# Moving a small expert product to the last group of heads, and its rows to the last three blocks

## The chip, the core and the metric

The kernel runs on one NeuronCore of a Trainium2 chip. Its engines work side by side, each through its own instructions in order: TensorE (PE in the profile; its weight loads are PEld), VectorE (DVE), ScalarE (ACT), GpSimd (POOL) and SyncE (SP, which only issues DMAs here). The metric is the device time of one execution in microseconds: 4233.94 us as the median of three runs, 4232.88 to 4234.31.

## The reference

The input x has 4 batches of 2048 tokens of 512 numbers. Its layer norm `xn` goes into two parts, and both are added to x:

```python
x = x + attention(xn) + experts(xn)

# attention: 16 heads of 32; q and k pass a filter over frequencies
scores = einsum('bhqd,bhkd->bhqk', q, k) / sqrt(32)
out = softmax(scores) @ v
attention = out @ w_out + b_out

# experts: each token goes to its best of 8, the first 100 tokens of each are kept
dispatched = einsum('tec,th->ech', dispatch, hs).reshape(800, 512)
expert_out = dispatched @ w_expert + b_expert     # one matrix for all experts
combined = combine.reshape(-1, 800) @ expert_out  # each row times its gate, back to its token
```

So the experts are 800 rows, 7 tiles of 128, through one 512 by 512 matrix. All else is attention in float32.

## The kernel before, in words

Heads are taken in groups of four; with four batches that makes 16 groups, k = 0 to 15 (group 12 is the first of the last batch). A group has four **blocks** of 512 queries, and a block has 16 **halves**, one for each tile of 128 keys. So there are 1024 halves, and `start = k * GH` with GH = 64 is the first half of group k. Two halves make a **window**.

In each half PE computes the scores of four heads (`scores`), ACT their exponentials into a tile `even` or `odd`, and PE the product of the half before with the values (`products`), which DVE adds to `num`. The row maxima must be known ahead: PE also computes the scores of a later block (`max_matmuls`), DVE reduces them (`max_reduce`, to `part`). These run 20 halves ahead, so that the last 20 halves have none. When the maxima of a block are complete, `max_negate` (DVE), `max_close` (PE and ACT) and `max_split` (POOL, tiles `rest` and `row`, then three DMAs on SP to `negm`) make a row of shifts from them, and `shift` puts it into the score banks at half 0 of the block, with PE products of `negm`. In a window the order is: `max_split` if due, then `heads` (the `divide` of a block: POOL computes `ot` from `num` and `factor`), then `pair` (a DMA on POOL's queue that adds the tile `odd` to `even`, 1 MB), then `add_to` (the sums of an older window, two additions on POOL, or on DVE when no maxima are left), then the two halves.

Everything else is laid into an **agenda** of halves: `at(half, step, cost=...)`. The cost counts PE work in units of one **piece**, a projection of 128 tokens (`query_key` or `value`): 32 instructions of 128*32 with 128 columns, in four column tiles, evicted by ACT. Each group makes the projections of the next one, 48 pieces, and `spread` places them in order, each as early as it may, while the sum of costs stays under a level times the number of halves; it takes the lowest level that fits. Pieces of keys (`kinds == 1`) may not stand before half 32 of a group. `projections(k)` sets their order; for k in CROWDED, which is (1, 14), two blocks of values and one of queries come first, 12 pieces, and then the keys. After each block `close_steps` puts a `fold` in half 5 of the next block, eight reciprocals (`invert`, DVE) in halves 6 to 13, the divide at half 14, four `result` products in halves 1 to 4 of the block after, and in half 5 the DMA that adds `y`, 1 MB, to `out`. For the last block but one they are placed earlier: fold in half 7, the divide and the results from half 12. The last block loads its rows of `out` into `y` (SP) and stores their sums at the end (`close_last`).

The experts (`expert_steps`, from `place_experts`) begin in half 36 of group 12: the matrix `w_exp`, the bias `b_exp` and the tables of chosen tokens are loaded, each row tile is fetched by an indirect DMA on POOL's queue, measured (DVE) and scaled. From half 62 of group 12 on, every second half holds an `expert(i)`: PE multiplies a turned tile by the matrix (four products of 128 by 128, 512 columns), DVE adds the bias, PE turns the next tile, ACT copies, weighs and normalizes. Their costs, 35 in all, mostly stand in group 13. From half 26 of group 13 on there is one row tile a block: `gather_row` reads its rows of `out` (an indirect DMA), `add_row` adds the expert's rows to them on POOL, and `scatter_row` writes them back, two halves apart. All POOL work, DMA issues too, is in program order (`InOrder`), and semaphores order reads and writes of `out`: a gather waits for the landing of the `y` added before it.

Of the kernel before, what the change touches and what calls it, by code (L numbers as in the profile page):

```python
# [21 lines left out]
B, S, DM = 4, 2048, 512  # L22
# [81 lines left out]
def attention_and_top1_experts(ctx: ExitStack, tc: tile.TileContext, a: dict, out: bass.AP):  # L104
# [7 lines left out]
    out_rows = out.rearrange("b s d -> (b s) d")  # L112
# [6 lines left out]
    def bank():  # L119

        return array[:, next(turns), :]
# [20 lines left out]
    ident, upto, same_head = (square[:, j, :] for j in range(3))  # L142
# [47 lines left out]
    on = SimpleNamespace(sync=nc.sync)  # L190
# [227 lines left out]
    def columns(out, lhsT, rhs, **flags):  # L418

        for h in range(HG):  # L420
            at = slice(DH * h, DH * (h + 1))
            on.tensor.matmul(out[at], lhsT=lhsT[:, at], rhs=rhs, **flags)
# [127 lines left out]

    taken = {}

    def expert_steps():


        def begin():
            w_exp = chunk("w_exp")
            on.sync.dma_start(out=w_exp, in_=a["L0_ffn_w_expert"].rearrange("(r p) n -> p r n", p=P))
            b_exp = work.tile([P, DM], F32, tag="b_exp", name="b_exp", bufs=1)
            on.sync.dma_start(out=b_exp, in_=a["L0_ffn_b_expert"].partition_broadcast(P))  # L560
            entries = small.tile([P, NTAB, ST, 2], F32, name="entries")
# [12 lines left out]
            mv = small.tile([P, ST, 2], F32, name="mv1")  # L574
            index = [bass.IndirectOffsetOnAxis(ap=who[:, i : i + 1], axis=0) for i in range(ST)]
            bound = {"bounds_check": B * S - 1, "oob_is_err": False}
            taken.update(mv=mv, w_exp=w_exp, b_exp=b_exp, entry=entry, index=index, bound=bound, xg=xg)

        def row(i):
            return taken["xg"][i // TQ][:, i % TQ, :]  # L580

        def fetch(i):
            on.gpsimd.indirect_dma_start(row(i), None, rows, taken["index"][i], **taken["bound"])

        def measure(i):
            stats = small.tile([P, 6], F32, name="stats1")
            on.vector.bn_stats(stats, row(i))
            on.vector.bn_aggr(taken["mv"][:, i, :], stats)

        def scale():  # L590
            rstd = small.tile([P, ST], F32, name="rstd1")
            on.gpsimd.tensor_scalar(rstd, taken["mv"][:, :, 1], EPS, None, ALU.add)
            on.gpsimd.tensor_tensor(rstd, rstd, power[:, 0:ST], ALU.pow)
            shift = small.tile([P, ST], F32, name="shift1")
            on.gpsimd.tensor_tensor(shift, taken["mv"][:, :, 0], rstd, ALU.mult)
            on.gpsimd.tensor_scalar(shift, shift, -1.0, None, ALU.mult)
            taken.update(rstd=rstd, shift=shift)

        def expert(i):

            if i >= 2:
                at = slice(i - 2, i - 1)
                pe = bank()
                for r in range(NR):
                    on.tensor.matmul(
                        pe,
                        lhsT=taken["xt"][:, r * P : (r + 1) * P],
                        rhs=taken["w_exp"][:, r, :],
                        start=(r == 0),
                        stop=(r == NR - 1),  # L610
                    )
                on.vector.tensor_tensor(row(i - 2), pe, taken["b_exp"], ALU.add)
            if 1 <= i <= ST:
                px = bank()
                for r in range(NR):
                    on.tensor.transpose(px[:, r * P : (r + 1) * P], row(i - 1)[:, r * P : (r + 1) * P], ident)
                taken["xt"] = work.tile([P, QB], F32, tag="byx", name="xt", bufs=1)
                on.scalar.copy(taken["xt"], px)
            if i >= 2:
                on.scalar.activation(row(i - 2), row(i - 2), AF.Copy, scale=taken["entry"][:, at, 1])  # L620
            if i < ST:
                at = slice(i, i + 1)
                on.scalar.activation(
                    row(i), row(i), AF.Identity, bias=taken["shift"][:, at], scale=taken["rstd"][:, at]
                )

        return begin, fetch, measure, scale, expert

    def gather_row(i):
        taken["sum"] = work.tile([P, DM], F32, tag="byx", name="yg", bufs=1)  # L630
        on.gpsimd.indirect_dma_start(taken["sum"], None, out_rows, taken["index"][i], **taken["bound"])

    def add_row(i):
        row = taken["xg"][i // TQ][:, i % TQ, :]
        on.gpsimd.tensor_tensor(row, row, taken["sum"], ALU.add)

    def scatter_row(i):
        row = taken["xg"][i // TQ][:, i % TQ, :]
# [105 lines left out]
    load, measure, scale, normalize, turn, first_route, first_sums, _ = token_stage(0)  # L744
# [8 lines left out]
    for c in range(1, NG):  # L753
        cols = slice(2 * DM + c * P, 2 * DM + (c + 1) * P)
# [63 lines left out]
    for i, item in enumerate(stream[:MAX_AHEAD]):  # L818
# [4 lines left out]
        half = next(turns), next(turns)  # L823
# [16 lines left out]
    HB = NT  # L840
    GH = NQ * HB
# [49 lines left out]
    def place_experts(start):  # L891


        begin, fetch, measure, scale, expert = expert_steps()
        first = start + 36
        at(first, begin)
        for i in range(ST):
            at(first + 2 + 2 * i, fetch, i)
            at(first + 6 + 2 * i, measure, i)
        at(first + 22, scale)  # L900
        for i in range(ST + 2):
            at(first + 26 + 2 * i, expert, i, cost=(NR if i >= 2 else 0) + (1 if 1 <= i <= ST else 0))
        for i in range(ST):
            free = start + GH + i * HB + 26
            for step in (gather_row, add_row, scatter_row):
                at(free, step, i)
                free += 2

    def plan(k):

# [86 lines left out]
    for block in range(1, B * NG * NQ):  # L997

        costs[block * HB - 4] += 0.25
    place_experts((B - 1) * NG * GH)  # L1000
    for k in range(B * NG):
        plan(k)

# [104 lines left out]
```

## Time and profile before

| | us |
|---|---|
| median of three runs | 4233.94 |
| profiled execution, its own time | 4234.09 |
| span of that execution in the trace | 4232.3 |
| PE busy | 4175.4 |
| DVE busy | 3453.9 |
| POOL busy | 2958.5 |
| ACT busy | 2489.9 |

Busy times are shares of the span in which an engine executed something; matmuls are pipelined, so a busy PE is not PE at its peak. The chain of waits follows the work that ended last, back from the last instruction, to what released it each time. A group of instructions has one line, with engine, operation, output and inputs, shapes, count, and mean duration. Nearly all instructions carry one line number, that of a helper, so that they are told apart by their tiles. A stage is a window of time from the span's start, and the windows below are cut at halves: a half begins where ACT starts the first of its two exponentials.

### The profile page before, as it was taken

To read this page: it belongs to the slowest core of one execution; us is meant where nothing else is said; L and a number is where in the kernel's file an instruction comes from. 1 tells how busy PE (TensorE), PEld (TensorE's weight loads), DVE (VectorE), ACT (ScalarE), POOL (GpSimd) and SP (SyncE) were. 2 spreads that over 40 slices of the span, in tenths; PEclk is the share of its full clock that TensorE was granted. 3 is DMA by queue.
4 is the path that set the end of the run, shared out by engine and by line. 5 is a ranking of instruction groups with operands and counts; after the bars stand their busy time and mean duration, and the time that the engine had idled before them with its cause. 6 is when DMAs were issued, how large, how long until landed. Compare 5 with 4: busy or idle time off the path is not lost.

```text
span 4232.3 us, 120483 instructions
## 1 busy us (share of the span) xinstructions
PE 4175.4 (99%) x52270; PEld 1866.6 (44%) x52270; DVE 3453.9 (82%) x5199; ACT 2489.9 (59%) x3411; POOL 2958.5 (70%) x2046
## 2 busy tenths in 40 slices
PE   8999999999999999999999999999999999999998
PEld 4444444444444444444444444444444443444432
DVE  6778888977788888897788888888778888788896
ACT  2555556666565556657565556566656555556665
POOL 1567776776876767776687767767678776677873
PEclk9999999999999999999999999999999999999999
DMA  4767788987787778898677787798777976778788
GB/s 120 154 128 150 157 159 170 209 195 149 142 163 153 156 156 166 181 203 185 134 158 156 157 160 152 159 204 195 166 149 147 182 159 132 152 162 163 157 170 170
DMA packets 183419, 685.95 MB, mean 162 GB/s; under 512 B 26902, under 2 KB 56760, under 8 KB 117608
## 3 DMA queue, kind: packets, MB, share of 16 engines
q0 software_dynamic: 110432, 605.83, 73.0%
q1 hardware_dynamic: 71280, 71.90, 5.5%
q8 instruction: 409, 6.70, 0.6%
q14 instruction: 122, 1.00, 0.1%
q10 hardware_dynamic: 1176, 0.52, 0.0%
HBM read 71.85 MB, written 88.96 MB: 38 GB/s over the span
## 4 chain that ended last, share of the span: by engine, by line
PE 88%; DMA 5%; POOL 3%; DVE 2%; issue 1%; ACT 0%; POOLq 0%; ACTq 0%; DVEq 0%
PE array L84 88%; DMA even<-odd 4%; POOL even L84 2%; DVE part L84 1%; POOL rstd L84 0%; DVE stats L84 0%; DVE num L84 0%; POOL ot L84 0%; DMA odd<-in_L_attn_w_qkv_dram 0%; DVE factor L84 0%; POOL steps_of_keys L84 0%; DMA negm<-row 0%; POOL rest L84 0%; POOL row L84 0%; ACT odd L84 0%
## 5 line engine op out<-in xcount | busy, mean ns | idle before, releaser
L84 DVE TENSOR_REDUCE part<-array 128x1 f32<-128x512 f32 (+1 forms) x3369 | 2496.5, 799 | 675.7 <-PE array L84 671.1
L84 POOL TENSOR_TENSOR even<-even 128x1024 f32<-128x1024 f32 x876 | 2111.2, 2500 | 458.4 <-DMA even<-odd 456.3
L84 PE MATMUL array<-keys,q 32*128 32x512 f32 x8192 | 2085.4, 616 | 8.5 <-DVE part L84 4.9
L84 PE MATMUL array<-q,steps_of_keys 32*128 32x512 f32 x8192 | 2038.9, 618 | 3.6 <-issue 2.1
L84 ACT ACTIVATE odd<-array 128x1024 f32<-128x1024 f32 x1024 | 996.2, 1021 | 489.0 <-PE array L84 366.0
L84 ACT ACTIVATE even<-array 128x1024 f32<-128x1024 f32 x1024 | 995.3, 1022 | 487.3 <-PE array L84 447.5
L84 PEld LDWEIGHTS array<-keys,q 32*128 32x128 f32 x8192 | 787.3, 185 | 583.2 <-DVE part L84 352.5
L84 PEld LDWEIGHTS array<-q,steps_of_keys 32*128 32x128 f32 x8192 | 704.8, 184 | 255.3 <-issue 225.1
L84 POOL DMA_DIRECT2D even<-odd x510 | 456.1, 894 | 436.3 <-ACT odd L84 369.0
L84 DVE TENSOR_TENSOR num<-num,array 128x512 f32<-128x512 f32 x960 | 650.3, 677 | 21.9 <-PE array L84 15.8
L84 PEld LDWEIGHTS array<-xnT,w 128*32 128x32 f32 x15808 | 444.6, 110 | 259.5 <-DVE part L84 165.0
L84 PE MATMUL array<-even,v 128*32 128x512 f32 x4096 | 547.0, 606 | 1.2 <-DVE part L84 1.2
L84 PE MATMUL array<-odd,v 128*32 128x512 f32 x4096 | 547.7, 607 | 0.3 <-DVE part L84 0.3
L84 PE MATMUL array<-xnT,w 128*32 128x128 f32 (+1 forms) x15808 | 522.2, 277 | 0.9 <-ACT xnT L84 0.7
L84 PEld LDWEIGHTS array<-w,xnT 128*32 128x32 f32 x8192 | 230.7, 110 | 146.4 <-DVE part L84 103.5
L84 DVE RECIPROCAL factor<-den 128x64 f32<-128x64 f32 x504 | 274.3, 545 | 0.0
L84 PE MATMUL array<-wo,ot 128*32 128x512 f32 x2048 | 267.1, 594 | 5.0 <-POOL ot L84 5.0
L84 PE MATMUL array<-w,xnT 128*32 128x128 f32 x8192 | 269.3, 273 | 1.3 <-DVE num L84 1.2
L84 PEld LDWEIGHTS array<-odd,v 128*32 128x32 f32 x4096 | 81.0, 108 | 391.2 <-DVE part L84 382.2
L84 PEld LDWEIGHTS array<-even,v 128*32 128x32 f32 x4096 | 80.7, 108 | 391.2 <-DVE part L84 381.4
L84 POOL DMA_DIRECT2D out_dram<-y x63 | 85.3, 1354 | 198.2 <-ACT y L84 126.7
L84 ACT COPY y<-array 128x512 f32<-128x512 f32 x188 | 110.0, 585 | 104.2 <-PE array L84 104.1
(129 smaller groups left out, 1437.5 us busy)
## 6 DMA issues: line engine op xcount, KB each, us to landing
even<-odd POOLq DMA_DIRECT2D x510, 1024.0 KB, 8.1
out_dram<-y POOLq DMA_DIRECT2D x63, 1024.0 KB, 9.8
xs<-in_L_attn_x_dram SPq DMA_DIRECT2D x96, 256.0 KB
out_dram<-in_L_attn_x_dram SPq DMA_DIRECT2D x16, 1024.0 KB
w<-wd SPq DMA_DIRECT2D x45, 256.0 KB
wo<-in_L_attn_w_out_dram SPq DMA_DIRECT2D x16, 256.0 KB
negm<-row SPq DMA_DIRECT2D x192, 4.0 KB
xs<-in_L_attn_x_dram SPq DMA_DIRECT2D x2, 1024.0 KB
```

The source lines that it names most:

```text
L84: done = act(*args, **kwargs)
```

## The change

The experts' product moves from groups 12 and 13 to group 15, the last. It begins in half 34 of group 14. The product of a tile is cut into four quarters of 128 columns, each done as `columns`, four column tiles, in a half of its own; the turn of a tile has its own half too. The halves used are those of group 15 without other products: not halves 1 to 5 of a block. Seven tiles of five halves each take 35 of them: halves 0 and 6 to 15 of blocks 0, 1 and 2, and halves 0 and 6 of block 3. The turned tile lies in buffers of projection weights that group 15 no longer needs. Rows are gathered, added and scattered in halves 8, 10 and 12 of blocks 1 (two tiles), 2 (two tiles) and 3 (three tiles), with a buffer for each gathered tile of a block.

```diff
+    def spent_weights(s):
+        return weights.tile([P, NR, P], F32, name=f"w{s}", bufs=1).rearrange("p r n -> p (r n)")
+
+    def spare_row():
+        return work.tile([P, DM], F32, tag="byx", name="yg", bufs=1)
...
-        def expert(i):
-
-            if i >= 2:
-                at = slice(i - 2, i - 1)
-                pe = bank()
-                for r in range(NR):
-                    on.tensor.matmul(
-                        pe,
-                        lhsT=taken["xt"][:, r * P : (r + 1) * P],
-                        rhs=taken["w_exp"][:, r, :],
-                        start=(r == 0),
-                        stop=(r == NR - 1),
-                    )
-                on.vector.tensor_tensor(row(i - 2), pe, taken["b_exp"], ALU.add)
...
+        def normal(i):
+            at = slice(i, i + 1)
+            on.scalar.activation(
+                row(i), row(i), AF.Identity, bias=taken["shift"][:, at], scale=taken["rstd"][:, at]
+            )
+
+        def turn(i):
+            px = bank()
+            for r in range(NR):
+                on.tensor.transpose(px[:, r * P : (r + 1) * P], row(i)[:, r * P : (r + 1) * P], ident)
+            taken["xt"] = spent_weights(i % 2)
+            on.scalar.copy(taken["xt"], px)
+
+        def multiply(i, quarter):
+            cols = slice(quarter * P, (quarter + 1) * P)
+            pe = bank()[:, cols]
+            for r in range(NR):
+                columns(
+                    pe,
+                    taken["xt"][:, r * P : (r + 1) * P],
+                    taken["w_exp"][:, r, cols],
+                    start=(r == 0),
+                    stop=(r == NR - 1),
                 )
+            on.vector.tensor_tensor(row(i)[:, cols], pe, taken["b_exp"][:, cols], ALU.add)
+
+        def weigh(i):
+            on.scalar.activation(row(i), row(i), AF.Copy, scale=taken["entry"][:, i : i + 1, 1])
...
     def gather_row(i):
-        taken["sum"] = work.tile([P, DM], F32, tag="byx", name="yg", bufs=1)
-        on.gpsimd.indirect_dma_start(taken["sum"], None, out_rows, taken["index"][i], **taken["bound"])
+        taken["sum", i] = spare_row() if i % 2 else spent_weights(2 if i < ST - 1 else 1)
+        on.gpsimd.indirect_dma_start(taken["sum", i], None, out_rows, taken["index"][i], **taken["bound"])
...
-        first = start + 36
+        begin, fetch, measure, scale, normal, turn, multiply, weigh = expert_steps()
+        first = start - 30
         at(first, begin)
         for i in range(ST):
             at(first + 2 + 2 * i, fetch, i)
             at(first + 6 + 2 * i, measure, i)
         at(first + 22, scale)
-        for i in range(ST + 2):
-            at(first + 26 + 2 * i, expert, i, cost=(NR if i >= 2 else 0) + (1 if 1 <= i <= ST else 0))
+        halves = iter([start + h for h in range(GH) if not 1 <= h % HB <= TQ + 1])
         for i in range(ST):
-            free = start + GH + i * HB + 26
-            for step in (gather_row, add_row, scatter_row):
-                at(free, step, i)
-                free += 2
+            half = next(halves)
+            at(half - 2, normal, i)
+            at(half, turn, i, cost=0.5)
+            for quarter in range(NR):
+                half = next(halves)
+                at(half, multiply, i, quarter, cost=1)
+            at(half + 1, weigh, i)
+        for block, tiles in ((1, (0, 1)), (2, (2, 3)), (3, (4, 5, 6))):
+            for step, half in ((gather_row, 8), (add_row, 10), (scatter_row, 12)):
+                for i in tiles:
+                    at(start + block * HB + half, step, i)
...
-    place_experts((B - 1) * NG * GH)
+    place_experts((B * NG - 1) * GH)
```

More of the change, by code (lines that the diff above doesn't have):

```diff
@@ L597, in scale @@
             taken.update(rstd=rstd, shift=shift)
-        def expert(i):
-            if i >= 2:
-                at = slice(i - 2, i - 1)
-                pe = bank()
-                for r in range(NR):
-                    on.tensor.matmul(
-                        pe,
-                        lhsT=taken["xt"][:, r * P : (r + 1) * P],
-                        rhs=taken["w_exp"][:, r, :],
-                        start=(r == 0),
-                        stop=(r == NR - 1),
-                    )
-                on.vector.tensor_tensor(row(i - 2), pe, taken["b_exp"], ALU.add)
[L613 to L624, printed above, removed]
-                )
@@ L627, in expert_steps @@
-        return begin, fetch, measure, scale, expert
+        def normal(i):
[9 more added lines that the diff above has]
+            on.scalar.copy(taken["xt"], px)
@@ L629, in gather_row @@
+        def weigh(i):
+            on.scalar.activation(row(i), row(i), AF.Copy, scale=taken["entry"][:, i : i + 1, 1])
+        return begin, fetch, measure, scale, normal, turn, multiply, weigh
     def gather_row(i):
-        taken["sum"] = work.tile([P, DM], F32, tag="byx", name="yg", bufs=1)
-        on.gpsimd.indirect_dma_start(taken["sum"], None, out_rows, taken["index"][i], **taken["bound"])
+        taken["sum", i] = spare_row() if i % 2 else spent_weights(2 if i < ST - 1 else 1)
+        on.gpsimd.indirect_dma_start(taken["sum", i], None, out_rows, taken["index"][i], **taken["bound"])
@@ L633, in add_row @@
     def add_row(i):
         row = taken["xg"][i // TQ][:, i % TQ, :]
-        on.gpsimd.tensor_tensor(row, row, taken["sum"], ALU.add)
+        on.gpsimd.tensor_tensor(row, row, taken["sum", i], ALU.add)
     def scatter_row(i):
@@ L891, in place_experts @@
     def place_experts(start):
-        begin, fetch, measure, scale, expert = expert_steps()
-        first = start + 36
+        begin, fetch, measure, scale, normal, turn, multiply, weigh = expert_steps()
+        first = start - 30
         at(first, begin)
```

## The prediction

> **What bounds the kernel now.** First the page's busy times and its chain of work, for the whole span.
>
> ```profile
> PE 4175.4 (99%) x52270; PEld 1866.6 (44%) x52270; DVE 3453.9 (82%) x5199; ACT 2489.9 (59%) x3411; POOL 2958.5 (70%) x2046
> ...
> PE 88%; DMA 5%; POOL 3%; DVE 2%; issue 1%; ACT 0%; POOLq 0%; ACTq 0%; DVEq 0%
> PE array L84 88%; DMA even<-odd 4%; POOL even L84 2%; DVE part L84 1%; POOL rstd L84 0%; DVE stats L84 0%; DVE num L84 0%; POOL ot L84 0%; DMA odd<-in_L_attn_w_qkv_dram 0%; DVE factor L84 0%; POOL steps_of_keys L84 0%; DMA negm<-row 0%; POOL rest L84 0%; POOL row L84 0%; ACT odd L84 0%
> ```
>
> TensorE bounds it, but an average hides the stages the change touches. So I took the start of the first exponential of each half as its beginning (two per half, 1024 halves) and asked for busy times by stage: groups 9, 12, 13, 14 and 15 (columns: window, length, then busy time and count of PE, PEld, DVE, ACT, POOL, granted clock, DMA share, GB/s).
>
> ```profile
> 2431.40:2681.30 249.90, 249.46 (x3261) 110.72 (x3256) 212.21 (x311) 147.25 (x200) 178.43 (x118) 1.00 0.80 157
> 3207.60:3459.30 251.70, 250.04 (x3264) 110.39 (x3256) 217.62 (x334) 147.84 (x201) 199.88 (x138) 1.00 0.83 167
> 3459.30:3743.60 284.30, 284.08 (x3343) 127.73 (x3340) 216.06 (x331) 160.40 (x220) 193.44 (x129) 1.00 0.73 146
> 3743.60:3992.70 249.10, 248.66 (x3260) 110.94 (x3256) 207.54 (x310) 151.72 (x208) 189.88 (x127) 1.00 0.81 162
> 3992.70:4232.30 239.60, 224.30 (x1658) 75.28 (x1650) 184.69 (x288) 143.81 (x162) 140.71 (x99) 0.99 0.84 168
> ```
>
> Group 9 has group 13's work without experts: the experts cost about 34.4 us there, and 1.8 in group 12 (groups 4 and 8 took 250.0). Group 15 has no projections; its four blocks:
>
> ```profile
> 3992.70:4049.10 56.40, 56.40 (x434) 20.70 (x430) 51.05 (x87) 35.84 (x40) 43.29 (x30) 1.00 0.80 159
> 4049.10:4105.80 56.70, 56.30 (x436) 20.49 (x430) 51.23 (x85) 35.91 (x41) 43.91 (x30) 1.00 0.86 170
> 4105.80:4163.80 58.00, 54.22 (x402) 18.49 (x398) 45.45 (x72) 35.45 (x40) 41.93 (x28) 0.98 0.82 163
> 4163.80:4232.30 68.50, 57.39 (x400) 15.60 (x392) 36.96 (x46) 36.61 (x42) 11.57 (x13) 0.97 0.85 178
> ```
>
> In blocks 0 and 1 a half without a piece takes 3.05 to 3.45 us and DVE is the chain; with one piece (group 14) it takes 3.75 to 3.85. That is the slack the experts move into. But POOL is 77% busy there, in order, and the last piece of the chain of waits runs through it:
>
> ```profile
> 4143.68 8.42 DMA even<-odd
> ...
> 4154.57 2.36 POOL even L84
> 4156.93 0.38 POOL rest L84
> ...
> 4181.60 15.58 DMA even<-odd
> ...
> 4202.63 2.02 POOL ot L84
> 4204.65 0.04 issue
> 4204.70 17.69 PE array L84 x128
> ```
>
> At the end of block 2 the maxima's split (rest) stands behind POOL's additions, which stand behind a pair transfer; PE then waits 3.79 us for negm (4157.35 to 4161.14). In block 3 PE waits 3.29 us for ot at half 12.
>
> **Removed from groups 12 and 13.** The planner spreads group 14's 48 pieces over group 13, under a level, around fixed costs. Key pieces may not stand before half 32, and CROWDED (not changed) puts only 12 pieces ahead of them. With the experts' cost of 35 in the way the blocks got 1, 6, 20 and 21 pieces. Without it, by the same formula, 12, 0, 25 and 11: the 25 as four in half 32, four in 36, eight in 40, five in 44, four after. Prices: block 0 as group 9's block 0, which has the same list, 62.6 us (was 84.0); block 1 without pieces, its own halves 0 to 11 (42.7) and group 15's last four (14.3), 57.0 (was 60.8); block 3 as group 9's, 61.7 (was 70.0). Block 2: 56.6 empty; the first piece of a half costs 0.1 to 0.8 and each further 0.88 (3.79 to 4.67; four in one half of group 11 made 6.47), together 19.2, so 75.9 (was 69.5). Sum 257.2 against 284.3: -27.1. Without the bunching it would be -34.4. Fetch, statistics and memsets leave group 12 (-1.8) and come to group 14 (+2.2: the same, and one more 0.68 us statistic beside a reciprocal). Their loads held SP for 18 us (3325 to 3343); at the new place SP's next work, negm, is due 12 halves later, so nothing. The seven fetches (1.1 us each on POOL) are in the 1.8. The early gathers, additions and scatters hid under POOL's slack in groups 13 and 14; I credit nothing.
>
> **Added to group 15.** A quarter has the shape of a query piece (128x32, 128 columns): 32 instructions, 0.87 us of PE, as the old product did over four quarters (3.44). A turn is four transposes, 0.53 us (3473.49 to 4.02). The DVE addition over 128 columns is bounded by 0.17 (a quarter of 0.69) and 0.69; I take 0.25, by the ratio of POOL's divides (0.46 over 128x128, 1.25 over 128x512). Normal (0.80), copy (0.58) and weighing (0.72) hide in ACT's waits for PE: it is 64% busy. Without that cover they cost 2.1 us a tile, 15 in all.
> - Block 0: eight quarters and three turns. From the halves of group 14 against 15: 0.74 + 3x0.41, 0.41 + 0.06 + 0.83 + 0.5 for quarters, 0.5 for turns, so 4.3; 0.7 for DVE at 3.65 of 3.8 us. +5.0.
> - Block 1: PE alone +5.1. POOL also gets two gathers, additions and scatters, from these rows:
>
> ```profile
> L84 POOL DMA_INDIRECT yg<-out_dram,who x7: 1097/1101/1130, 3587.0 to 3974.2; - x7
> L84 POOL TENSOR_TENSOR xg<-xg,yg x7: 1277/1587/1601, 3593.7 to 3981.8; 128x512 f32<-128x512 f32 x7
> L84 POOL DMA_INDIRECT out_dram<-xg,who x7: 1088/1088/1092, 3603.3 to 3991.9; - x7
> ```
>
>   2x(1.10 + 1.59 + 1.09) = 7.5 us. All stand before the split of the block's maxima. The second scatter writes the same tensor as the first; I take it that it waits for the landing (3.6 us less the 1.09 of issue: +2.5), because every gather in the trace waits for the landing of the y add before it; the other end is 0. POOL's only idle time after half 8 is 0.67, so the split comes 9.3 later, and 0.35 from PE; it had 1.4 to spare. PE would start block 2 at +5.1, waits to +8.3, and I add 0.4 for data traffic: +8.7.
> - Block 2: the same 10.0 us on POOL, less 2.2 idle (4149.9 to 4152.1): split +7.8 with 0.35 of PE, so +8.1. The quarters after half 10 fall into the 3.79 us stall; PE alone would be +6.7 - 3.79.
> - Block 3: three gathers stand behind the y add of half 5 (landed 4192.29) and in the queue behind pairs landing at 4197.2 and 4202.1. At 4.9 us a megabyte (4197.18 to 4202.06) each takes 1.2: landed by 4205.7. POOL's three additions (1.6 each) then end at 4208.2, and the divide behind them, which began at 4202.60, comes 5 us later, result and all behind it too. Two quarters and traffic +1. The three scatters land one after another, by about 4224.5; only then may SP load y (6.4 us, 4160.25 to 4166.64), which was needed at 4225.79 and now at 4231.5: just covered. +6.7, between 0 (gathers overtake the pairs) and 16.
> - The granted clock: after the 3.79 us wait the page's stages show 0.94, a half clock for 3.4 us, 1.7 us of work; after 4.92 us of idleness at 2934 it lasted 6.8. Longer waits at three places: 0 to 5, I take 1.7.
>
> [...]
>
> Sum: -27.1 - 1.8 + 2.2 + 5.0 + 8.7 + 8.1 + 6.7 + 1.7 = +3.5 us. The profiled execution took 4234.09 us (span 4232.3), 0.15 from the median 4233.94: about 4237.5.
>
> **Rivals.** (1) Faster: row work costs POOL less than PE's slower pace gives back. For it: one row set a block went unseen in group 14. Scatters do not wait for each other and gathers pass the pairs. Then blocks cost 5.0, 5.1, 2.9 and 1.5: -12.2, 4221.7. It decides where block 1's split is under 6.5 us late. Against it: 7.5 us of work and 0.67 of idle time.
> (2) Slower: the last block's row traffic ends the kernel. If each scatter waits behind a 1 MB pair (4.9 us), the last lands near 4231 instead of 4224.5, y arrives 6 us after it is needed, and the additions wait for gathers 3 longer: +9 on the sum, 4246.5. It decides when the last scatter lands after about 4225 of the old time. For it: the queue ran full from 4175 to 4207 (15.58 us for a transfer of median 8.1).
> (3) Slower: DVE bounds blocks 0 and 1. If an addition costs 0.69, halves of 3.4 become 4.1 against 3.8: 15x0.3 more, with the same delay in reciprocals near the end: +5 to +8, 4243 to 4246.
> (4) Bunching costs nothing in group 13 (-34.4): 4230, still no change.
>
> **How the numbers follow.** 0.2% is 8.5 us, about what a measurement of this kernel can tell from no change: 4225.5 to 4242.4. The forecast with (4) has 0.45; (1) 0.20; (2) and (3) 0.35, as more of the bounds lie above than below. The range leaves out half of (1) and the far end of (2) with a long half clock: 4223 to 4252. The likeliest case alone: 4229 to 4243.
>
> **What would show it.** Group 13 near 257 us with a half of about 10 us (eight pieces) in block 2; group 12 at 250; group 15's blocks near 61, 65, 66 and 77. PE's waits for negm at blocks 2 and 3 of 3 to 5 us, one for ot of 8. Split behind scatters on POOL. Wrong if negm isn't awaited at block 2 (then 1), if y's load ends after its first addition is due (2), or if DVE is idle-free in block 0 (3).

## The result, and the profile after

The changed kernel takes 4247.78 us (median of 12 runs, 4242.32 to 4254.88) against 4233.88 us for the kernel before on the same chip (12 runs, 4231.18 to 4237.36): a ratio of 1.0034 [1.0026, 1.0042], 13.9 us slower. The forecast was 4237.5, the range reached to 4252. The profiled execution of the changed kernel took 4248.93 us, its span is 4247.1.

The page gives less this time: its chain was followed back over one per cent of the span only.

```profile
PE 4169.8 (98%) x53110; PEld 1876.8 (44%) x53110; DVE 3458.5 (81%) x5195; ACT 2490.0 (59%) x3411; POOL 2963.0 (70%) x2046
...
PE 1%; POOL 0%; DVE 0%; issue 0%; DVEq 0%; POOLq 0%
```

TensorE is busy for 5.6 us less than before, and the span is 14.8 us longer: the loss is not more work for it. Where it is shows in the stages, groups 12 to 15 (columns as before the change: window, length, busy time and count of PE, PEld, DVE, ACT, POOL, granted clock, DMA share, GB/s):

```profile
3204.70:3454.70 250.00, 249.56 (x3261) 110.39 (x3256) 212.62 (x317) 147.36 (x200) 190.09 (x127) 1.00 0.80 158
3454.70:3719.80 265.10, 259.71 (x3261) 117.73 (x3256) 211.09 (x328) 148.86 (x201) 178.67 (x118) 0.99 0.75 148
3719.80:3978.20 258.40, 250.78 (x3260) 111.07 (x3256) 216.19 (x326) 152.55 (x209) 191.57 (x130) 0.99 0.81 162
3978.20:4247.10 268.90, 242.40 (x2582) 95.99 (x2574) 190.45 (x288) 153.22 (x182) 165.85 (x119) 0.96 0.79 162
```

Before, groups 13 and 14 ran at a clock of 1.00 with PE idle for 0.2 and 0.4 us. Now PE idles for 5.4 and 7.6 us in them. Against the prediction:

| | before | predicted | after | predicted change | measured change |
|---|---|---|---|---|---|
| group 12 | 251.8 | 250.0 | 250.0 | -1.8 | -1.8 |
| group 13 | 284.3 | 257.2 | 265.1 | -27.1 | -19.2 |
| group 14 | 249.1 | 251.3 | 258.4 | +2.2 | +9.3 |
| group 15 | 239.6 | 269.8 | 268.9 | +30.2 | +29.3 |

The four measured changes sum to +17.6. The rest, -2.9, is in groups 0 to 11, whose code did not change: over the twelve profiled executions of this study they took between 3201 and 3210 us, so a few microseconds there mean nothing. Two terms are off, by +7.9 and +7.1 us; the large one in group 15 holds.

**Group 13.** The prediction gave the half with eight pieces about 10 us. It took 14.9, and block 2 84.2 instead of 75.9. The timeline of PE (start, duration, operation, and in brackets the idle time before it with what ended it) has three gaps in that block that end with no event at all:

```profile
3580.12 0.41 PE L84 MATMUL array<-xnT,w 128*32 128x128 f32 x3 [0.98 <-issue]
...
3601.05 0.41 PE L84 MATMUL array<-xnT,w 128*32 128x128 f32 x3 [1.90 <-issue]
...
3621.63 4.92 PE L84 MATMUL array<-w,xnT 128*32 128x128 f32 x108 [2.52 <-issue]
```

Each gap is inside a row of pieces: two halves of four and the half of eight. No wait that the profile knows ended there. The DMA queue that the page names `instruction` has 16 KB fetches, about 1 us each, that begin at 3577.9, 3598.7 and 3619.3: each gap ends 2.2 to 2.4 us after one of them. So do all the gaps of this kind over 0.5 us in the twelve profiles, 26 from 110 us on. The kernel before has one of them too. The keys of group 1 are crowded as well (`CROWDED`), and the half of group 0 with four of their pieces takes 10.25 us:

```profile
242.42 1.08 PE L84 MATMUL array<-q,steps_of_keys 32*128 32x512 f32 x4 [2.06 <-issue]
```

The prediction took its price for a bunch from group 11 and did not count this one. In the changed kernel the clock is halved after the longest gap of group 13 (windows of the same columns):

```profile
3618.30:3621.60 3.30, 0.82 (x28) 0.55 (x19) 0.00 (x0) 0.27 (x1) 0.00 (x0) 1.00 0.03 5
3621.60:3625.10 3.50, 3.47 (x68) 3.47 (x71) 0.00 (x0) 0.53 (x2) 0.00 (x0) 0.52 0.02 5
3625.10:3628.50 3.40, 3.40 (x68) 2.00 (x64) 0.86 (x2) 1.25 (x3) 0.00 (x0) 0.99 0.02 5
```

Gaps of 5.4 us and 1.7 us of work lost to the half clock (half of 3.4) make 7.1 of the 8.3 us that the block is over its forecast.

**Group 14.** Nearly the whole loss, 8.5 of 9.3 us, is half 3 of block 2, 12.3 us long where it took 3.8 before. The timeline there:

```profile
3855.44 4.93 POOL L84 TENSOR_TENSOR even<-even 128x1024 f32<-128x1024 f32 x2
...
3857.04 0.31 DVE L84 TENSOR_REDUCE entry<-entries 128x7 f32<-128x28 f32 x2 [1.65 <-DMA entries<-table]
3857.28 6.18 DVE L84 CAST who<-entry 128x7 int32<-128x7 f32 x1
3860.03 3.41 POOL L84 MEMSET xg<- 128x2048 f32 x2
...
3863.54 0.20 PEld L84 LDWEIGHTS array<-even,v 128*32 128x32 f32 x8 [7.37 <-DVE part L84]
3863.54 1.94 PE L84 MATMUL array<-even,v 128*32 128x512 f32 x8 [6.54 <-DVE part L84]
```

The conversion of seven token numbers a partition to integers, a small operation on DVE, is in progress for 6.18 us. It ends at 3863.46, 0.03 us after POOL has finished its two additions and the two memsets of the new tiles, which follow each other without a gap. In the kernel before the same operation took 0.82 us and ended 0.03 us after one memset. Behind it stands a maximum over scores on DVE, and PE waits 6.54 us for that; the clock is then half for 6.8 us.

**Group 15.** Its four blocks:

```profile
3978.20:4039.60 61.40, 61.31 (x702) 26.41 (x698) 52.98 (x83) 39.26 (x47) 46.42 (x31) 1.00 0.80 156
4039.60:4105.60 66.00, 62.77 (x730) 27.32 (x726) 53.42 (x88) 38.60 (x47) 47.20 (x33) 0.98 0.74 151
4105.60:4173.20 67.60, 59.54 (x698) 24.90 (x694) 46.27 (x71) 38.46 (x46) 49.77 (x35) 0.95 0.77 157
4173.20:4247.10 73.90, 58.78 (x464) 17.37 (x461) 37.78 (x48) 36.91 (x43) 22.46 (x22) 0.92 0.84 182
```

Forecast were 61.4, 65.4, 66.1 and 75.2, and 1.7 for the clock. PE's three long waits are the three forecast ones:

```profile
4103.06 0.61 PE L84 MATMUL array<-negm,ones_b 3*128 3x512 bf16 x4 [3.23 <-DMA negm<-row]
...
4170.80 0.62 PE L84 MATMUL array<-negm,ones_b 3*128 3x512 bf16 x4 [8.01 <-DMA negm<-row]
...
4217.28 1.94 PE L84 MATMUL array<-wo,ot 128*32 128x512 f32 x8 [7.30 <-POOL ot L84]
```

And POOL's own rows at the end of block 1 show the cause: the second scatter waits 2.57 us for the first to land, and the split (`rest`, `row`) stands behind it.

```profile
4095.09 1.08 POOL L84 DMA_INDIRECT out_dram<-xg,who  x1 [0.18 <-POOL even L84]
4098.74 1.02 POOL L84 DMA_INDIRECT out_dram<-xg,who  x1 [2.57 <-DMA out_dram<-xg,who]
4099.77 0.42 POOL L84 TENSOR_TENSOR rest<-rest,row 16x128 f32<-16x128 f32 x1
```

### The profile page after: what moved, and what is told of

Same layout as the page of the kernel before. It is cut to its first block, busy times and chain, and to the rows that moved or that the text cites. A ratio compares the mean times of both kernels' runs of the same rounds, so it can differ in the third digit from the quotient of the medians.

```text
span 4247.1 us, 122155 instructions
## 1 busy us (share of the span) xinstructions
PE 4169.8 (98%) x53110; PEld 1876.8 (44%) x53110; DVE 3458.5 (81%) x5195; ACT 2490.0 (59%) x3411; POOL 2963.0 (70%) x2046
```

## The experiments

The theory after the result has three parts: bunched pieces make PE stand in group 13, as I read it for want of instructions (265.1 against 249.9 us in group 9, 8 of these 15 not forecast); the conversion on DVE waits for POOL in group 14 (7 us); and the rows' work on POOL delays the maxima in group 15 (some 15 us). Each has a rival: the 15 us in group 13 could be the pieces' own work, the 7 us in group 14 a late table, and group 15's loss could come from PE's slower pace alone.

**Keys spread in group 13** (`e1_order`). The order of group 14's projections is the normal one again, so the pieces of keys are not pressed together.

```diff
-CROWDED = (1, (B - 1) * NG + 2)
+CROWDED = (1,)
```

> The changed kernel with CROWDED = (1,), so that group 14's projections stand in the usual order (all values and two blocks of queries ahead of the keys). Theory (the kept order bunches 25 pieces into block 2 of group 13): the pieces spread to 12, 12, 13 and 11, group 13 goes from 265.1 us to about 250, and the time from 4247.8 to 4232 or 4233. Rival (group 13 is long for another reason, the moved experts' traffic for instance): group 13 stays above 260 and the time above 4244.

Measured: 4232.99 us against 4232.71, ratio 1.0002 [0.9992, 1.0011]. Group 13 and group 14, in the same windows as above:

```profile
3454.20:3704.00 249.80, 249.36 (x3260) 110.47 (x3256) 212.54 (x317) 147.12 (x200) 178.75 (x118) 1.00 0.80 158
3704.00:3962.90 258.90, 251.43 (x3261) 111.17 (x3256) 216.47 (x326) 152.33 (x209) 191.65 (x130) 0.99 0.81 161
```

Group 13 has the same PE work (3260 matmul records against 3261) in 15.3 us less, and group 14 keeps its loss. So the whole of group 13's excess over group 9 belongs to the order of the pieces.

**The conversion on ACT** (`e2_cast`).

```diff
-            on.vector.tensor_copy(who, entry[:, :, 0])
+            on.scalar.copy(who, entry[:, :, 0])
```

> The changed kernel with one conversion, that of the tokens' numbers to integers (who<-entry), on ACT and not on DVE. Theory (DVE's conversion, 6.2 us long in group 14, is held up until POOL's additions and memsets end, and all DVE work and PE behind it): the half of 12.3 us in block 2 of group 14 becomes about 4, and the time falls by 8 to 10 us to 4238 to 4240. Rival (the half is long because the tables land late, and whoever reads them waits): ACT waits in its place, the half stays over 10 us and the time within 3 us of 4247.8.

Measured: 4238.39 us, ratio 1.0015 [1.0006, 1.0025]. The conversion takes 0.20 us on ACT, and the longest half falls to 5.36 us, where about 4 was expected; group 14 is 251.5 us, and 251.3 was forecast for the changed kernel. The tables are no earlier in this run: DVE waits 2.2 us for them, against 1.65 in the changed kernel. So in the changed kernel a late table is not what cost the 7 us.

**The rows left out** (`e3_norows`). Gathers, additions and scatters are not done, so the output lacks the experts' rows.

```diff
-        for block, tiles in ((1, (0, 1)), (2, (2, 3)), (3, (4, 5, 6))):
-            for step, half in ((gather_row, 8), (add_row, 10), (scatter_row, 12)):
-                for i in tiles:
-                    at(start + block * HB + half, step, i)
```

> The changed kernel without gathers, row additions and scatters: the experts' rows are computed and not added to the output. Theory (the rows' work on POOL, 7.5 us a block and the waits between scatters, delays the maxima's split and the last divide): group 15 falls from +29 us against the kernel before to +14 or +15 (blocks about 61, 62, 61 and 70), the time to 4232 to 4234. Rival (the quarters on PE and DVE make most of it): group 15 keeps +24 or more, the time stays above 4242.

Measured: 4230.2 us, ratio 0.9992 [0.9982, 1.0001], below the expected 4232 to 4234. The blocks of group 15:

```profile
3979.20:4040.60 61.40, 61.31 (x702) 26.41 (x698) 52.97 (x83) 39.20 (x48) 46.72 (x31) 1.00 0.81 158
4040.60:4102.20 61.60, 61.60 (x730) 26.77 (x726) 53.38 (x88) 38.61 (x47) 43.55 (x28) 1.00 0.79 155
4102.20:4160.20 58.00, 57.95 (x697) 24.65 (x690) 44.56 (x70) 38.30 (x46) 38.21 (x26) 1.00 0.80 157
4160.20:4228.20 68.00, 58.13 (x466) 16.67 (x464) 38.94 (x50) 36.86 (x43) 12.08 (x14) 0.97 0.85 177
```

With the quarters and turns alone, group 15 is 9.5 us longer than before, not the expected 14 or 15: 5.0 and 4.9 in blocks 0 and 1, nothing in blocks 2 and 3, where 3 and 1.5 were expected. PE waits nowhere for `negm`. It fills in block 2 the stall that the kernel before had there. So the rows are worth 19.8 us of group 15's 29.3.

**The rows alone** (`e4_rows`). The kernel before, its expert product where it was, with only the rows' steps and their buffers moved.

```diff
-        for i in range(ST):
-            free = start + GH + i * HB + 26
-            for step in (gather_row, add_row, scatter_row):
-                at(free, step, i)
-                free += 2
+        last = (B * NG - 1) * GH
+        for block, tiles in ((1, (0, 1)), (2, (2, 3)), (3, (4, 5, 6))):
+            for step, half in ((gather_row, 8), (add_row, 10), (scatter_row, 12)):
+                for i in tiles:
+                    at(last + block * HB + half, step, i)
```

> The kernel before with only its rows moved: gathers, additions and scatters in blocks 1 to 3 of group 15 as in the changed kernel, the experts' product still in groups 12 and 13. Theory (the rows hold POOL, whoever else works): PE is not slowed by quarters there and waits more, about 8 us at block 2, 8 at block 3 and 5 to 8 at the last divide: 4253 to 4258, a ratio of 1.0045 to 1.0057. Rival (the rows hide in POOL's 25% of idle time and cost only beside the quarters): 4234 to 4238.

Measured: 4254.97 us, ratio 1.0055 [1.0038, 1.0072], the slowest of all. PE's longest waits in group 15 are those for `negm` (total, times, longest):

```profile
PE array L84 <- DMA negm<-row: 18.1, 2, 10.3
...
POOL out_dram L84 <- DMA out_dram<-xg,who: 9.5, 4, 2.6
```

Blocks 1, 2 and 3 are 8.7, 7.7 and 4.7 us longer than before. The two parts of the change do not add: 9.5 for the product and 21.1 for the rows make 30.6, close to the 29.3 of both, but the waits for `negm` are 18.1 us here and 11.2 there. PE, slowed by the product, arrives later at a split that comes hardly later: blocks 1 and 2, which end soon after it, take 65.4 and 65.7 us here, 66.0 and 67.6 with the product.

**At most two pieces in a half** (`e5_two`). Same order as in the changed kernel, but the planner puts no more than two of the pieces in one half of group 13.

```diff
-    def spread(steps, last):
+    def spread(steps, last, most=99):
...
-                while half < first or done + cost / 2 > level * (half - base + 1):
+                while half < first or found.count(half) >= most or done + cost / 2 > level * (half - base + 1):
...
-            done = spread(steps, last)
+            done = spread(steps, last, 2 if k == 13 else 99)
```

> The changed kernel with one more rule for the spread in group 13: at most two pieces in a half (block 2 then has 24 pieces, two in most halves, in place of 4, 4, 8 and 5 at once). The unequal load of the blocks stays. Theory (a half with four or eight pieces uses up PE's instructions faster than they are fetched, and PE waits with no other releaser): no such wait of over 1 us in group 13, block 2 takes 73 to 76 us in place of 84.2, the time falls to 4237 to 4241. Rival (the unequal load alone costs it, blocks without pieces being slowed by DVE): block 2 stays above 81 and the time above 4244.

Measured: 4236.83 us, ratio 1.0011 [1.0001, 1.0021], just under the expected 4237 to 4241. Block 2 takes 74.1 instead of 84.2, its longest half 5.54, and PE has no gap of over half a microsecond that ends without an event. One of the 25 pieces has moved to block 3, which is 0.9 us longer for it. The 48 pieces of group 13 are the same, and the group falls from 265.1 to 255.9 us, so 9.2 us were the price of placing them in fours, a five and an eight; the remaining 6 against `e1_order` is having 24 of them in one block and none in the one before.

**Scatters to tensors of their own** (`e6_apart`). The second scatter of blocks 1 and 2, and the last two of block 3, write to other DRAM tensors, so that of each block only the first reaches `out`.

```diff
+    apart = [dram1.tile([B * S, DM], F32, name=f"apart{i}") for i in range(2)]
...
-        on.gpsimd.indirect_dma_start(out_rows, taken["index"][i], row, None, **taken["bound"])
+        to = out_rows if i in (0, 2, 4) else apart[i == 6]
+        on.gpsimd.indirect_dma_start(to, taken["index"][i], row, None, **taken["bound"])
```

> The changed kernel with the second scatter of blocks 1 and 2, and the second and third of block 3, written to tensors of their own, so that no scatter writes what the one before it writes. Those rows don't reach the output. All instructions stay. Theory (a second scatter waits for the landing of the first, 2.6 and 3.3 us of POOL ahead of the maxima's split): the split comes earlier by that, PE's waits for negm go from 3.2 to about 0.7 and from 8.0 to about 4.7, and the time falls by 5 to 6 us to 4241 to 4243. Rival (the DMA queue is what delays the split, and the wait moves to the next instruction): PE's waits stay within 1 us and the time within 3 us of 4247.8.

Measured: 4243.13 us, just over the expected 4241 to 4243, ratio 1.0026 [1.0016, 1.0035], from 1.0034 [1.0026, 1.0042]. The intervals overlap, so it is the profile that shows what changed. In POOL's waits the landing of a scatter is gone; PE's wait for `negm` falls from 3.23 to 0.94 us at block 2 but only from 8.01 to 6.81 at block 3, which was expected to fall further.

```profile
PE array L84 <- POOL ot L84: 8.3, 2, 6.6
PE array L84 <- DMA negm<-row: 7.7, 2, 6.8
...
POOL apart L84 <- issue: 1.2, 4, 0.3
```

So the order between scatters to one tensor is real and costs PE about 2.3 us at the first place. At the second the split begins 2.7 us earlier in its block, 59.1 us after the block's start against 61.9. But one of its four operations took 1.17 us instead of 0.28, and PE came 0.6 us earlier in the block, so that only 1.2 us of the gain reach PE.

This run holds one more thing. The long half of group 14 is there (12.5 us), but with a conversion of 0.23 us; instead DVE waited for a table, from 3857.0 to 3864.1, and the conversion ended 0.03 us after POOL's last memset again.

```profile
DVE entry L84 <- DMA entries<-table: 7.1, 1, 7.1
```

The DMA records show that this table did land late: the queue of its packets of 4 and 8 bytes moved 116 of them from 3858.0 to 3862.5, beside 113 packets of a pair transfer, and the last 238 in the 1.1 us after that. In the changed kernel none of the table's packets comes after 3857.0. So that half can be long by about the same for two reasons, and the rival of `e2_cast`, the late table, is true of this run though not of the changed kernel.

**Scatters behind the split** (`e7_behind`). Keys spread, conversion on ACT, and in blocks 1 and 2 the scatters come in half 14, behind the maxima's split.

```diff
...
-            for step, half in ((gather_row, 8), (add_row, 10), (scatter_row, 12)):
+            for step, half in ((gather_row, 8), (add_row, 10), (scatter_row, 14 if block < 3 else 12)):
```

> The changed kernel with the usual order of group 14's projections, the conversion on ACT, and the scatters of blocks 1 and 2 in half 14 in place of 12, behind the split of the maxima. Theory (what stands ahead of the split on POOL is what delays it): the split of both blocks comes 4 to 6 us earlier, PE doesn't wait at block 2 and under 4 us at block 3, so 8 us on top of the 15 and 9 of the two other edits: 4213 to 4220, faster than the kernel before. Rival (the scatters then hold up the pair transfers behind them, and block 3 pays it back): the first three blocks are shorter and the last one longer by as much, 4222 to 4226.

Measured: 4224.45 us, ratio 0.9987 [0.9977, 0.9996]: not the expected 4213 to 4220, but the rival's 4222 to 4226. Block 1 takes 61.6, as without rows, and the wait at block 2 is gone. At block 3 PE still waits 5.22 us for `negm`, where under 4 was expected: POOL reached the gathers of block 2 only 42.7 us after the block's start (39.1 in the changed kernel), after a wait of 5.47 us for a pair transfer (3.84). Block 3 is now 79.7 (73.9 in the changed kernel): its `y` add lands 16.6 us after its issue and the gathers start only then, and PE waits for ACT, which waits 5.1 us for a pair transfer to land.

```profile
4139.75 0.62 PE L84 MATMUL array<-negm,ones_b 3*128 3x512 bf16 x4 [5.22 <-DMA negm<-row]
4180.22 2.99 PE L84 MATMUL array<-q,steps_of_keys 32*128 32x512 f32 x8 [4.02 <-ACT odd L84]
4191.99 1.94 PE L84 MATMUL array<-wo,ot 128*32 128x512 f32 x8 [6.92 <-POOL ot L84]
```

Of the 7.5 us won in blocks 1 and 2 (4.4 and 3.1), the last block gives back 5.8. The clock is at half there for 17.1 us, from 4180.5 on.

**Three rows in block 2, two in block 3** (`e8_rows`). Keys spread, conversion on ACT, additions at half 14, scatters apart by two halves, in block 3 additions and scatters at half 12 behind the last divide, and the fifth tile moved from the last block to block 2, with a buffer that held output weights.

```diff
...
-        taken["sum", i] = spare_row() if i % 2 else spent_weights(2 if i < ST - 1 else 1)
+        if i == 4:
+            taken["sum", i] = weights.tile([P, DM], F32, name="wo")
+        else:
+            taken["sum", i] = spare_row() if i % 2 else spent_weights(2)
...
+        for block, tiles in ((1, (0, 1)), (2, (2, 3, 4)), (3, (5, 6))):
+            here = start + block * HB
+            for n, i in enumerate(tiles):
+                at(here + 8, gather_row, i)
+                at(here + (14 if block < 3 else 12), add_row, i)
+                at(here + (15 + 2 * n if block < 3 else 12), scatter_row, i)
```

> As the one before, with the rows laid out otherwise: tiles 0 and 1 in block 1, tiles 2, 3 and 4 in block 2, tiles 5 and 6 in block 3; additions behind the split (half 14) and scatters one at a time, in halves 15, 17 and 19 from the block's start; in block 3 additions and scatters behind the last divide (half 12). Theory: no PE wait for negm over 3 us, and the wait for ot at half 12 of block 3 back to 3 to 4 us from 7.3, so 4 to 8 us less than with the scatters alone: 4207 to 4214. Rival (the tail takes it back: y is loaded only when the last scatter has landed): a wait of 4 us or more ahead of the last additions, 4214 to 4222.

Measured: 4212.62 us against 4231.18, ratio 0.9955 [0.9938, 0.9972]: faster than both kernels. Block 3 takes 69.4, near the 68.0 without rows, and PE's wait for `ot` is 3.30 us, down from 7.30.

```profile
4138.02 0.61 PE L84 MATMUL array<-negm,ones_b 3*128 3x512 bf16 x4 [6.05 <-DMA negm<-row]
4182.11 1.94 PE L84 MATMUL array<-wo,ot 128*32 128x512 f32 x8 [3.30 <-POOL ot L84]
```

One part of what was expected did not come: no wait for `negm` over 3 us. At block 3 it is 6.05 us, although block 2's own additions and scatters stand behind the split. Ahead of it in the block are its three gathers, and early on two additions and two scatters that block 1 left. POOL also waited there for pair transfers:

```profile
4101.16 4.68 POOL L84 TENSOR_TENSOR even<-even 128x1024 f32<-128x1024 f32 x2 [4.08 <-DMA even<-odd]
...
4112.62 4.67 POOL L84 TENSOR_TENSOR even<-even 128x1024 f32<-128x1024 f32 x2 [5.99 <-DMA even<-odd]
```

Without rows (`e3_norows`) its longest wait of this kind in block 2 is 3.95 us. So at block 3 the split is late both for POOL's work ahead of it and for the DMA queue that the rows share with the pairs; no run parts the two.

**The memsets earlier, the conversion on DVE** (`e9_clear`). The tiles are cleared in a step of their own, four halves before the others.

```diff
+        def clear():
+            xg = [chunk("xg"), small.tile([P, ST - TQ, DM], F32, name="xg1")]
+            for half in xg:
+                on.gpsimd.memset(half, 0.0)
+            taken["xg"] = xg
...
-            xg = [chunk("xg"), small.tile([P, ST - TQ, DM], F32, name="xg1")]
-            for half in xg:
-                on.gpsimd.memset(half, 0.0)
+            xg = taken["xg"]
...
+        at(first - 4, clear)
```

> The changed kernel with the two memsets of the rows' tiles four halves earlier; the conversion of the tokens' numbers stays on DVE. Theory (DVE's conversion can't finish while POOL works without a gap; in the changed kernel it ended with the second memset): it now ends with the pair of additions that it meets, 2 to 4 us in place of 6.2, the half of 12.3 us becomes 6 to 9, and the time falls by 3 to 6 us to 4242 to 4245. Rival (the conversion is long by itself at this place, for the late tables): 6 us as before, and the time within 2 us of 4247.8.

Measured: 4247.34 us against 4236.75, ratio 1.0026 [1.0015, 1.0037]; by its time this run misses the expected 4242 to 4245. It is 10.6 us slower than the kernel before on the same chip, where the changed kernel was 13.9 slower, a gain that is not clear of the noise. By its profile it does what was said. The conversion, in the answer for the tile `who` (shortest, median and longest in ns; first and last start; shape), first the changed kernel, then this one:

```profile
L84 DVE CAST who<-entry x1: 6185/6185/6185, 3857.3 to 3857.3; 128x7 int32<-128x7 f32 x1
```

```profile
L84 DVE CAST who<-entry x1: 1094/1094/1094, 3858.4 to 3858.4; 128x7 int32<-128x7 f32 x1
```

It still waits, but for the one addition that is in progress, and ends 0.03 us after it, 2.3 us before the second addition of the pair ends. In the changed kernel it did not end between the two additions of a pair; why it did here isn't settled. Group 14 falls from 258.4 to 252.8. Block 3 is 2.9 us longer than in the changed kernel (76.8), which takes half of that back. Taking `xg` earlier can change which tile's buffer it inherits; whether that is why block 3 is longer was not tried.

**The best version again** (`e10_rows`), the same kernel as `e8_rows`, on another chip.

> The fastest of the kernels so far once more, with more rounds: usual order, conversion on ACT, rows as in the run with tiles 2, 3 and 4 in block 2. Theory: 4211 to 4214, a ratio to the kernel before between 0.994 and 0.997. Rival (its four runs were lucky ones): 4216 or more.

Measured: 4215.09 us against 4236.75, ratio 0.995 [0.9936, 0.9963]: a microsecond over the expected 4211 to 4214, with the ratio as expected. The gain holds. The two profiles of one kernel also show how far a single reading goes: PE's wait for `negm` at block 3 is 6.05 us in the first and 0.35 in the second, which has a wait of 2.34 us in block 3 instead, behind a pair transfer. A difference of some microseconds at one place is safe only where several kernels repeat it.

## Why the prediction was right, and where not

**The total.** +3.5 was forecast and +13.9 measured, outside the likeliest case's 4229 to 4243 and inside the range. The two slower rivals had 0.35. The loss came by neither of their mechanisms; it came from two terms on the side of groups 13 and 14. That it lies inside the range is luck: the upper part of the range stood for rival (2) with a long half clock, which did not come.

**Group 12, -1.8: right**, 250.0 as forecast.

**Group 13, -27.1: mis-sized, -19.2.** Blocks 0, 1 and 3 were forecast as 62.6, 57.0 and 61.7 and took 62.5, 56.8 and 61.6, and the matmuls of the four blocks make 12, 0, 25 and 11 pieces, as worked out. The step that failed is "the first piece of a half costs 0.1 to 0.8 and each further 0.88 (3.79 to 4.67; four in one half of group 11 made 6.47)". A price read in other bunches, of at most four pieces, was drawn on to eight, and it did not hold at four either: halves of four took 7.8 and 9.6 where that of group 11 took 6.47, the half of eight 14.9 where about 10 was forecast. `e5_two` shows that the excess goes when the pieces stand in twos. Rival (4), bunching for free, fell: bunching cost more than the sum had for it, not less. `e1_order` puts bunching and crowding together at 15.3 us.

That PE was short of instructions is the likeliest reading of gaps that end without an event, each 2.2 to 2.4 us after a 16 KB fetch began; it is not shown, as no run changed the fetches alone. Shown is that the gaps go with the bunches. If the gaps of 0.98, 1.90 and 2.52 us are the cost of those fetches, it is 5.4 us in block 2.

**Group 14, +2.2: mis-sized, +9.3.** The step was "come to group 14 (+2.2: the same, and one more 0.68 us statistic beside a reciprocal)": the operations were costed at their durations in group 12, where the conversion took 0.82 us. That duration was itself a wait for POOL, a short one, because the memset beside it was about to end. At the new place additions of 2.6 us each and memsets of 2.1 and 1.7 us follow one another, and the conversion waited for all. I had listed SP's queue for the moved step, but neither DVE's nor what POOL does beside it. `e2_cast` (another engine) and `e9_clear` (memsets elsewhere) both remove most of it, with group 14 at 251.5 and 252.8 us; in the changed kernel, `e1_order`, `e3_norows`, `e5_two` and `e9_clear` alike the conversion ends within 0.03 us of a POOL instruction.

The end of the conversion goes with POOL's work, not with a longer time of its own: in `e9_clear` its 1.09 us end with one addition, in the changed kernel its 6.18 us with the last of a row of POOL instructions. What in the chip holds it until then, no run shows.

**Group 15, +30.2: right in its sum, +29.3.** Block by block +5.0, +9.3, +9.6 and +5.4 were measured, and +5.0, +8.7, +8.1 and +6.7, with 1.7 for the clock, forecast. The sum is better than its parts, and that is luck. Rival (1) has the prices without the rows' delays, 5.0, 5.1, 2.9 and 1.5, which is 14.5 of the 30.2; `e3_norows` measured 5.0, 4.9, 0.1 and -0.5, which is 9.5. So the product was taken 5 us too dear, in blocks 2 and 3, and the rows, 15.7 with the clock, cost 19.8. DVE's addition over 128 columns took 0.227 us (taken: 0.25, bounds 0.17 and 0.69), so rival (3) fell. The second scatter waited for the first as taken: 2.57 and 3.34 us against 2.5. The reason given for it was not in the trace before, where each gather came 24.4 to 26.1 us after the issue of a `y` add that landed in 8.8 to 9.7, and POOL was idle for 0.2 us ahead of it; the changed kernel has one such wait, 1.6 us. The wait at block 2 was 3.23 against 3.2 (from +5.1 to +8.3), the one for `ot` 7.30 against 8. The wait at block 3 was 8.01, where 3 to 5 was named: 0.8 us of the miss is the scatter's, and PE's own work in block 2 grew by 3.7 us (57.95 us busy without rows, 54.22 before) and not by 6.7, so that PE came earlier and waited longer. Block 3 itself was shorter than forecast. Rival (1), rows for free, fell at the first `negm`; without rows at all (`e3_norows`) group 15 still grows by 9.5, and the total is just level. Rival (2), row traffic ending the kernel, fell too: the third scatter was issued at 4229.34, and the load of `y` began at 4231.69, in time for its additions.

**The clock, 1.7: somewhat low.** Waits of 3.23, 8.01 and 7.30 us were followed by half clocks of 3.4, 6.8 and 10.2 us:

```profile
4103.00:4106.50 3.50, 3.44 (x20) 1.34 (x20) 1.08 (x2) 0.92 (x1) 3.50 (x3) 0.51 0.87 176
4167.80:4174.70 6.90, 3.90 (x20) 1.12 (x24) 0.00 (x0) 1.48 (x2) 3.86 (x7) 0.51 0.59 134
4212.00:4222.30 10.30, 5.02 (x24) 1.12 (x28) 2.26 (x2) 1.56 (x3) 7.13 (x6) 0.51 0.64 130
```

In the second and third window PE is idle for 3.0 and 5.3 us, so half of the slow time fell into the waits themselves. PE was busy for 12.4 us at a clock of 0.51, by which 6.1 us of work were lost (0.49 of it), an estimate from the clock alone. Before, it lost 1.7 behind the wait at block 2 (3.46 us at 0.51) and 1.7 behind the one for `ot` (7 us at 0.76). So the term was 2.7 us. All three waits were followed by a slow clock, but so were shorter ones: in `e2_cast`, which has the same bunches in group 13, the clock halved after 1.86 us and not after 2.66 (PE's timeline, then the windows behind the two gaps).

```profile
3602.01 0.41 PE L84 MATMUL array<-xnT,w 128*32 128x128 f32 x3 [1.86 <-issue]
...
3624.39 2.83 PE L84 MATMUL array<-w,xnT 128*32 128x128 f32 x96 [2.66 <-issue]
...
3602.50:3606.00 3.50, 3.50 (x20) 1.04 (x24) 1.29 (x2) 1.25 (x2) 0.00 (x0) 0.51 1.07 196
3624.30:3627.80 3.50, 3.41 (x112) 3.21 (x115) 0.00 (x0) 0.92 (x4) 0.00 (x0) 1.00 0.02 5
```

In the changed kernel it was the other way round, after 2.52 us and not after 1.90. So no length between these tells whether the clock will halve.

## What to carry to other kernels

A small operation that is moved takes its neighbours along: before costing it by its old duration, look what the engines beside it do at the new place, and whether the old duration was already a wait. A price per piece read in one bunch need not hold in another, even with as many pieces: look for the worst bunch that the trace already has (here 10.25 us for four), and spread the pieces where that costs nothing. And where an engine works in order, put what nobody awaits (here the scatters) behind what the bound engine awaits (the maxima's split), and then look at what the last stage pays. A sum that comes out right is no proof of its terms: here two of group 15's were off by 4 to 5 us, one each way.

## What the runs showed of the hardware that I had not expected

- In long rows of short products TensorE stood for 0.98, 1.90 and 2.52 us with no wait that the profile knows, in halves of four and eight pieces, and not above 0.5 us with the pieces in twos. In twelve profiles 26 such gaps each ended 2.2 to 2.4 us after a 16 KB instruction fetch began; that it had run out of instructions is the likeliest reading, which no run shows.
- A gap of 2.52 us was followed by a half clock of 3.4 us (3621.7 to 3625.1), and after one of 1.90 us the clock stayed at 1.00; in `e2_cast` the half clock came after 1.86 us, and after 2.66 the clock stayed.
- A 128x7 conversion on VectorE took 0.23, 0.62, 0.82, 1.09, 5.78, 5.95, 6.18 and 6.41 us in different runs, each time until 0.03 us after a GpSimd addition or memset ended, the last of a gapless row in the long ones; on ScalarE it took 0.20.
- A scatter to a DRAM tensor waited for the landing of the scatter before it to the same tensor, 2.57 and 3.34 us in blocks 1 and 2; to a tensor of its own, 0.3.
- The queue of a table's packets of 4 and 8 bytes moved 116 of them in 4.5 us beside 113 packets of a 1 MB transfer, and 238 in the 1.1 us after that (`e6_apart`).
